# Two places instead of one for a block's token list and its indices

## The chip, the cores and the metric

The kernel runs on one core of a Trainium2 chip. The metric is the device time of one execution in microseconds (us).

## The reference, cut to what matters

A layer of deformable convolution attention is followed by a layer of linear attention with a mixture of experts. The change lies in the mixture of experts, the last part of the program: of four experts every token uses its best two.

```python
def _L1_ffn_ref(x, gate_w, gate_b, w1, b1, w2, b2):        # 4096 tokens of 384, 4 experts, 1536 hidden
    probs = softmax(einsum('bsd,de->bse', x, gate_w) + gate_b)
    topk_vals, topk_idx = top_k(probs, 2)
    mask = sum(one_hot(topk_idx, 4), axis=-2)
    masked = probs * mask
    masked = masked / (sum(masked, axis=-1, keepdims=True) + 1e-09)
    h = gelu(einsum('bsd,edh->ebsh', x, w1) + b1[:, None, None, :])
    y = einsum('ebsh,ehd->ebsd', h, w2) + b2[:, None, None, :]
    return einsum('bse,ebsd->bsd', masked, y)
...
t = t + _L1_ffn_ref(_ln_t(t), ...)
```

## The kernel before

The program has three stages. The first two are the convolution attention (to about 1390 us of the profile) and the linear attention with the gate (to about 1770 us). In `gate` each pair of a token and an expert gets a row of the table `tab_d` in DRAM, sorted by expert; a row holds the token's number to read from, the number to write to, and the gate's weight. The normalised tokens go to `tn_d`, the sum so far to `out`.

The third stage works on 25 blocks of rows of one expert each: 13 blocks of 512 rows, 3 of 256 and 9 of 128. `ORDER` says in which order: first ten long blocks, then two short ones (128 rows) and one long one in turn, then the rest. Which expert a block belongs to and where its rows begin is known only at run time; SP loads both from `btab`.

A block j passes through these steps:

- `fetch` (L1672) brings it in. SP issues, in this order, the loads of `en` (L1686, the rows of the table), w1 (L1700) and w2 (L1704, 2304 KB each), `b1c` (L1708) and `b2r` (L1710). POOL turns the first two columns of `en` into integers `ei` (L1690) and gathers the tokens `xr` with them by indirect DMA (L1693), 128 rows with each.
- `turn` (L1713) transposes the tokens: TensorE (`e_tr`, L1719), and VectorE copies the result to `d_xT` (L1722).
- `first_layer` (L2072) and the activation (L2079; for short blocks a copy, transposes `h_tr` and the activation, L2077, L2088 and L2092).
- `second_layer` (L2104) sums into PSUM banks `acc`, four for 512 rows. The pool has four banks.
- `rows_so_far` (L2117) gathers from `out` what these tokens have so far, by indirect DMA on POOL with `ei`, and VectorE adds the weighted bias (L2123, which reads `en` and `b2r`).
- `to_rows` adds the weighted result on VectorE (L2131, which reads `acc` and `en`) and POOL scatters the rows back to `out` (L2134, with `ei`). A token may have been written by a block before, so the gather at L2117 waits until the scatters of earlier blocks have landed.

There are three homes for blocks, (dw0, ds0), (dw1, ds1) and (dw2, ds2), used in turn. Each home has one place for every tile of `fetch`, so block j+2 takes over the places of block j-1. In the loop over the units (12 units of 128 hidden columns for a long block, 3 of 512 for a short one), `fetch` of block j+2 is written down in the second unit of block j (first unit if j is short), `turn` of block j+1 three units before the end of block j, and the first layer runs two units ahead of the second:

```python
                if u == (1 if n == HC else 0) and j + 2 < N_BLK:
                    ds[j + 2] = fetch(j + 2, *homes[(j + 2) % 3])
                if u == n - 3 and j + 1 < N_BLK:
                    turn(ds[j + 1], j + 1, d2p)
```

The order of instructions on each engine in this stage is set by a scheduler that goes by priorities and by when it expects operands and places to be free. Every engine then works off its own list in order, and waits at an instruction whose operands or whose place aren't ready; what stands behind it waits too.

Of the kernel before, what the change touches and what calls it, by code (L numbers as in the profile page):

```python
# [11 lines left out]
F32 = mybir.dt.float32  # L12
I32 = mybir.dt.int32
# [6 lines left out]
P = 128  # L20
# [131 lines left out]
def bc(ap, axis, n):  # L152

    dims = [list(d) for d in ap.ap]
    dims.insert(axis, [0, n])
    return bass.AP(ap.tensor, ap.offset, dims)
# [3 lines left out]
def body(  # L160
# [140 lines left out]
    with tc.tile_pool(name="a_w", bufs=1) as aw, tc.tile_pool(name="a_1", bufs=1) as a1, tc.tile_pool(  # L301
        name="a_2", bufs=2
    ) as a2, tc.tile_pool(name="a_3", bufs=2) as a3, tc.tile_pool(name="a_s", bufs=2) as asm, tc.tile_pool(
        name="a_cv", bufs=1, space=PSUM
    ) as pcv, tc.tile_pool(name="a_mm", bufs=2, space=PSUM) as pmm, tc.tile_pool(
        name="a_tr", bufs=3, space=PSUM
# [560 lines left out]
        def fetch(b, k):  # L867

            ga = a3.tile([P, G, 2, 2 * GC], F32, tag="ga", bufs=4, name=f"ga{b}_{k}")
            for g in range(G):  # L870
                nc.gpsimd.indirect_dma_start(  # L871
                    out=ga[:, g].rearrange("p s c -> p (s c)"),
                    out_offset=None,
                    in_=img[b][:, :],
                    in_offset=bass.IndirectOffsetOnAxis(
                        ap=pidxs[b, k][:, g : g + 1], axis=0
                    ),
                )
            gas[b, k] = ga
# [43 lines left out]
        for b in range(B):  # L923
# [56 lines left out]
            for f in range(2):  # L980
# [51 lines left out]
                for k in range(4 * f, 4 * f + 4):  # L1032
                    k0 = k // sizes[0] * sizes[0]
                    done = (k + 1) % sizes[0] == 0
                    step(
                        ("G", b, k), "Pool", 8.6, 1 + b + 0.01 * k, (lambda b=b, k=k: fetch(b, k)),
                        [("N", b, k0, 12), ("S", b, 16)] + [("rec", b, i) for i in range(2 * G)]
                        + [("G", b - 1, i) for i in range(NB) if b]
                        + [("G", b, i) for i in range(k0) if b == B - 2],
                        takes=[("ga", (b, k))], gives=[("pidx", (b, k0))] if done else [],  # L1040
                    )
                    step(("L", b, k), "queue", 0.0, 0, lambda: None, [("G", b, k)], lag=2.6)
                    step(
                        ("M", b, k), "DVE", 3.4, 2.2 + b, (lambda b=b, k=k: sampled(b, k)),
                        [("L", b, k), ("N", b, k0, 13)] + ([("M", b, k - 1)] if k % K4 else []),
                        takes=[(f"xs{b % 2}{f}", (b, f))] if k % K4 == 0 else [],
                        gives=[("ga", (b, k))] + ([("w4", (b, k0))] if done else []),
                    )
# [66 lines left out]
    with tc.tile_pool(name="b_w", bufs=1) as bwp, tc.tile_pool(name="b_qkv", bufs=2) as bq, tc.tile_pool(  # L1115
        name="b_win", bufs=4
    ) as bwin, tc.tile_pool(name="b_t", bufs=4) as bt, tc.tile_pool(name="b_o", bufs=2) as bo_, tc.tile_pool(
        name="b_s", bufs=6
    ) as bS, tc.tile_pool(name="b_m", bufs=2) as bm, tc.tile_pool(name="b_ao", bufs=1) as bao, tc.tile_pool(
        name="b_y", bufs=3  # L1120
# [377 lines left out]
        with tc.manual_schedule(  # L1498
# [22 lines left out]
            for g in range(NP + 7):  # L1521


                i, kp = divmod(g, KP)
# [51 lines left out]
            while waiting:  # L1576
                tag, n = spots.pop(0)
# [94 lines left out]
    def fetch(j, pool, small):  # L1672

        i = ORDER[j]
        b, size = blocks[i]
        why = "the table is made of clipped counts"
        e = nc.values_load(
            btab[0:1, i, 0:1], engines=SP, min_val=0, max_val=E_N - 1,
            skip_runtime_bounds_check_because=why,
        )  # L1680
        r = nc.values_load(
            btab[0:1, i, 1:2], engines=SP, min_val=0, max_val=ROWS - size,
            skip_runtime_bounds_check_because=why,
        )
        en = small.tile([P, 4, 4], F32, tag="en", name=f"en{i}")
        nc.sync.dma_start(  # L1686
            en[:, : size // P, :], tab_d[bass.DynSlice(r, size), :].rearrange("(p k) c -> p k c", p=P)
        )
        ei = small.tile([P, 4, 2], I32, tag="ei", name=f"ei{i}")
        nc.gpsimd.tensor_copy(ei[:, : size // P], en[:, : size // P, 0:2])  # L1690
        xr = small.tile([P, 4, NC], F32, tag="xr", name=f"xr{i}")
        for k in range(size // P):
            nc.gpsimd.indirect_dma_start(  # L1693
                out=xr[:, k, :],
                out_offset=None,
                in_=tn_d[: (b + 1) * N, :],
                in_offset=bass.IndirectOffsetOnAxis(ap=ei[:, k, 0:1], axis=0),
            )
        t1 = pool.tile([P, CK, HID], F32, tag="w1", name=f"w1_{i}")
        nc.sync.dma_start(  # L1700
            t1, w1[bass.DynSlice(e, 1)].rearrange("o (a p) d -> p (o a) d", p=P)
        )
        t2 = pool.tile([P, HC, NC], F32, tag="w2", name=f"w2_{i}")
        nc.sync.dma_start(  # L1704
            t2, w2[bass.DynSlice(e, 1)].rearrange("o (a p) d -> p (o a) d", p=P)
        )
        c1_ = small.tile([P, HC], F32, tag="b1c", name=f"b1c{i}")
        nc.sync.dma_start(c1_, b1_d[bass.DynSlice(e, 1)].rearrange("o p a -> (o p) a"))  # L1708
        r2 = small.tile([P, NC], F32, tag="b2r", name=f"b2r{i}")
        nc.sync.dma_start(r2, bc(b2[bass.DynSlice(e, 1)].rearrange("o c -> (o c)"), 0, P))  # L1710
        return dict(j=j, size=size, b=b, en=en, ei=ei, xr=xr, w1=t1, w2=t2, b1=c1_, b2=r2)
# [18 lines left out]
    with tc.tile_pool(name="c_1", bufs=1) as c1, tc.tile_pool(name="c_2", bufs=2) as c2, tc.tile_pool(  # L1730
        name="c_s", bufs=2
# [246 lines left out]
        def outputs(b):  # L1978
# [36 lines left out]
            if b == 1:  # L2015

                state["block"] = fetch(0, dw0, ds0)
# [36 lines left out]
    with tc.tile_pool(name="d_w1", bufs=1) as dw1, tc.tile_pool(name="d_s1", bufs=1) as ds1, tc.tile_pool(  # L2054
        name="d_w2", bufs=1
    ) as dw2, tc.tile_pool(name="d_s2", bufs=1) as ds2, tc.tile_pool(name="d_2", bufs=2) as d2p, tc.tile_pool(
        name="d_h", bufs=3
# [86 lines left out]

        homes = [(dw0, ds0), (dw1, ds1), (dw2, ds2)]
        ds = {0: first, 1: fetch(1, *homes[1])}
        units = []
        for j in range(N_BLK):
# [76 lines left out]
```

## Time and profile before

| | us |
|---|---|
| median of three runs | 2853.95 (2847.24 to 2855.77) |
| the profiled execution | 2848.14 |
| its span on the core | 2846.1 |
| TensorE busy | 2585.0 (91%) |
| VectorE busy | 1578.6 (55%) |
| ScalarE busy | 1158.2 (41%) |
| GpSimd (POOL) busy | 853.3 (30%) |

The profile is of one execution. Its own time is the span and what lies around it (2 us here), and is 5.8 us below the median of the three runs. Engines are PE (TensorE), PEld (its weight loads, which overlap PE), DVE (VectorE), ACT (ScalarE), POOL (GpSimd) and SP (SyncE, which only issues DMAs here). L1686 is line 1686 of the kernel. An arrow `ei<-en` gives output and input of an instruction; a bracket such as `[1.62 <-DMA xr<-tn_d,ei]` is the idle time of the engine before the instruction and what ended it. PEclk is the granted clock of TensorE as a share of full speed. The ends of matmuls are modelled; distances are better taken from start to start.

### The profile page before, as it was taken

How to read it: one execution, taken by the hardware profiler on the slowest of the kernel's cores; microseconds unless marked ns; L12 is line 12 of the kernel's file. 1: busy time of each engine (PE TensorE's matmuls, PEld its weight loads, DVE VectorE, ACT ScalarE, POOL GpSimd, SP SyncE). 2: the span in 40 equal slices, each digit the busy share in tenths (PEclk: the TensorE clock that was granted, in tenths of full speed). 3: DMA queues.
4: the chain of work that ended last, by engine and by line, in shares of the span. 5: the costliest groups of instructions: out<-in, count | busy, mean ns of one | idle time of the engine just before them, and what ended most of it. 6: DMA issues, size and time to landing. Idle time of an engine off the chain costs nothing. (4 is left out here: it accounts for less than half of the span.)

```text
span 2846.1 us, 33342 instructions
## 1 busy us (share of the span) xinstructions
PE 2585.0 (91%) x12731; PEld 1283.9 (45%) x12731; DVE 1578.6 (55%) x2349; ACT 1158.2 (41%) x1532; POOL 853.3 (30%) x776
## 2 busy tenths in 40 slices
PE   8899838898989988888799898999999999999999
PEld 5555512332333333233365554555555555555566
DVE  3888859999999999999656765000101011011011
ACT  5565536777667766676323322111111111111121
POOL 1668853232333333332112335211112111021121
PEclk9899969999999999999999999999999999999999
DMA  7934575454546555544121312622223434374371
GB/s 205 257 115 133 173 209 165 130 154 145 164 145 194 177 157 149 145 151 127 55 74 52 119 45 70 250 103 103 103 103 119 146 129 142 114 255 172 117 267 58
DMA packets 267899, 404.77 MB, mean 142 GB/s; under 512 B 134674, under 2 KB 207634, under 8 KB 267356
## 3 DMA queue, kind: packets, MB, share of 16 engines
q1 hardware_dynamic: 214912, 230.43, 25.6%
q0 software_dynamic: 52112, 172.15, 18.6%
q8 instruction: 100, 1.64, 0.2%
q14 instruction: 59, 0.48, 0.1%
q10 hardware_dynamic: 716, 0.07, 0.0%
HBM read 345.68 MB, written 70.06 MB: 146 GB/s over the span
## 5 line engine op out<-in xcount | busy, mean ns | idle before, releaser
L2072 PE MATMUL ph<-d_xT,w 128*128 128x512 f32 (+1 forms) x1152 | 484.1, 554 | 1.3 <-ACT h L2079 1.3
L2104 PE MATMUL acc<-w,h 128*128 128x384 f32 x1392 | 480.3, 486 | 0.0
L1168 POOL DMA_INDIRECT win<-table,widx x192 | 278.2, 1449 | 642.4 <-DVE t L1194 612.8
L1221 PE MATMUL ps<-q,k 64*64 64x512 f32 x1536 | 380.3, 608 | 91.6 <-DVE S L1252 43.4
L2079 ACT ACTIVATE h<-ph,b1c 128x512 f32<-128x512 f32 (+1 forms) x192 | 124.2, 647 | 776.2 <-PE ph L2072 761.7
L1226 PE MATMUL ps<-o,ident 64*64 64x512 f32 x1536 | 376.6, 609 | 9.4 <-ACT o L1202 9.4
L2104 PEld LDWEIGHTS acc<-w,h 128*128 128x128 f32 x1392 | 264.1, 190 | 208.5 <-issue 73.2
L2072 PEld LDWEIGHTS ph<-d_xT,w 128*128 128x128 f32 x1152 | 217.0, 191 | 196.3 <-issue 144.5
L871 POOL DMA_INDIRECT ga<-img,pidx x192 | 233.3, 1215 | 145.7 <-DVE gd L600 62.5
L2134 POOL DMA_INDIRECT out<-rows,ei x67 | 67.2, 1003 | 699.4 <-DVE rows L2131 690.5
L1315 ACT ACTIVATE S<-S 128x2048 f32<-128x2048 f32 x96 | 183.4, 1910 | 190.3 <-DVE S L1311 190.3
L1221 PEld LDWEIGHTS ps<-q,k 64*64 64x64 f32 x1536 | 98.8, 133 | 354.4 <-issue 211.3
L1722 DVE COPY d_xT<-e_tr 128x512 f32<-128x512 f32 (+2 forms) x75 | 36.6, 512 | 385.5 <-PE e_tr L1719 385.5
L1194 DVE SCALAR_TENSOR_TENSOR t<-win,bw,t 128x1056 f32<-128x1056 f32 x192 | 244.5, 1314 | 5.1 <-ACT t L1184 3.9
L1252 DVE SCALAR_TENSOR_TENSOR S<-t,bw,ps 128x1024 f32<-128x1024 f32 x192 | 236.9, 1275 | 17.4 <-PE ps L1226 14.3
L2123 DVE SCALAR_TENSOR_TENSOR rows<-b2r,en,rows 128x384 f32<-128x384 f32 x67 | 40.7, 618 | 361.3 <-DMA rows<-out,ei 311.1
L1184 ACT ACTIVATE t<-win,bw 128x1056 f32<-128x1056 f32 x192 | 218.1, 1168 | 40.3 <-DMA win<-table,widx 39.2
L1202 ACT ACTIVATE o<-t,bw 128x1024 f32<-128x1024 f32 x192 | 212.8, 1144 | 35.2 <-DVE t L1194 30.0
L1329 PE MATMUL po<-S,v 128*64 128x512 f32 x768 | 199.0, 642 | 24.4 <-ACT av L1354 13.9
L1311 DVE TENSOR_TENSOR S<-S,pbs 128x2048 f32<-128x2048 f32 x96 | 218.9, 2282 | 2.0 <-ACT pbs L1306 2.0
L2131 DVE SCALAR_TENSOR_TENSOR rows<-acc,en,rows 128x384 f32<-128x384 f32 x67 | 41.4, 618 | 217.6 <-PE acc L2104 215.7
L1270 DVE TENSOR_TENSOR m<-m,S 128x2048 f32<-128x2048 f32 x48 | 117.1, 2440 | 1.6
(350 smaller groups left out, 3441.8 us busy)
## 6 DMA issues: line engine op xcount, KB each, us to landing
w<-in_L_ffn_w SPq DMA_DIRECT2D x50, 2304.0 KB
img<-in_x SPq DMA_DIRECT2D x48, 256.0 KB
q<-q_d SPq DMA_DIRECT2D x48, 256.0 KB
x<-in_x SPq DMA_DIRECT2D x8, 768.0 KB
q_d<-qt SPq DMA_DIRECT2D x24, 256.0 KB
v_d<-qkvw SPq DMA_DIRECT2D x32, 192.0 KB
v<-v_d SPq DMA_DIRECT2D x24, 256.0 KB
k<-k_d SPq DMA_DIRECT2D x48, 128.0 KB
```

What stands on the lines that cost most here:

```text
L871: nc.gpsimd.indirect_dma_start(out=ga[:, g].rearrange("p s c -> p (s c)"), out_offset=None, in_=img[b][:, :], in_offset=bass.IndirectOffse ...
L1168: nc.gpsimd.indirect_dma_start(out=win, out_offset=None, in_=tables[h // 2][:, :], in_offset=bass.IndirectOffsetOnAxis(ap=widx[b][:, nb, h ...
L1184: nc.scalar.activation(t.rearrange("p y x -> p (y x)"), wins[p, e][:, : HI * WIN], AF.Copy, scale=weight(p, e, 0),)
L1194: nc.vector.scalar_tensor_tensor(tf, wins.pop((p, e))[:, WIN:], weight(p, e, 1), tf, ALU.mult, ALU.add)
L1202: nc.scalar.activation(o, ts[p, e][:, :, 0:WI], AF.Copy, scale=weight(p, e, 2))
L1221: made.append(nc.tensor.matmul(ps[HALF[1 - r], e, FULL[f]], k[HALF[r], 2 * kp + e, :], q[HALF[r], FULL[f]], start=(step == 0), stop=(step ...
L1226: made.append(nc.tensor.matmul(ps[HALF[r], d, FULL[f]], ident[HALF[r], HALF[r]], os_[p, d][HALF[r], FULL[f]], start=(step == 0), stop=(ste ...
L1252: nc.vector.scalar_tensor_tensor(st[:, e, :].rearrange("p (y x) -> p y x", x=WI), ts.pop((p, e))[:, :, 1:WIN], weight(p, e, 3), ps[:, e, : ...
L1311: nc.vector.tensor_tensor(Ss[p], Ss[p], bc(pbss[p // KP][:, :], 1, 2), ALU.add)
L1329: nc.tensor.matmul(pos[i][0][HALF[f], :], vs[i][:, 2 * kp + e, :], Ss[p][:, e, FULL[f]], start=(first and e == 0), stop=(last and e == 1),)
L2072: nc.tensor.matmul(ph if short(d) else ph[:, :n], a, m, start=(c == 0), stop=(c == CK - 1))
L2104: nc.tensor.matmul(d["acc"][0 if short(d) else s][:, :NC], h[:, s * P : (s + 1) * P], d["w2"][:, hc, :], start=(hc == 0), stop=(hc == HC - 1),
```

## The change

In `fetch`, the tiles `en` and `ei` get two places in each home instead of one. Everything else in a home (`xr`, w1, w2, `b1c`, `b2r`) keeps its one place. A home's `en` takes 64 bytes a partition and `ei` 32 bytes.

```diff
@@ fetch
-        en = small.tile([P, 4, 4], F32, tag="en", name=f"en{i}")
+        en = small.tile([P, 4, 4], F32, tag="en", bufs=2, name=f"en{i}")
         nc.sync.dma_start(
             en[:, : size // P, :], tab_d[bass.DynSlice(r, size), :].rearrange("(p k) c -> p k c", p=P)
         )
-        ei = small.tile([P, 4, 2], I32, tag="ei", name=f"ei{i}")
+        ei = small.tile([P, 4, 2], I32, tag="ei", bufs=2, name=f"ei{i}")
         nc.gpsimd.tensor_copy(ei[:, : size // P], en[:, : size // P, 0:2])
         xr = small.tile([P, 4, NC], F32, tag="xr", name=f"xr{i}")
         for k in range(size // P):
```

With two places, block j+2 uses the place that block j-4 had, while block j-1 keeps its own.

## The prediction

> **What bounds the kernel now.** I read the page first: busy shares, then the forty slices.
>
> ```profile
> PE 2585.0 (91%) x12731; PEld 1283.9 (45%) x12731; DVE 1578.6 (55%) x2349; ACT 1158.2 (41%) x1532; POOL 853.3 (30%) x776
> PE   8899838898989988888799898999999999999999
> ```
>
> TensorE has the largest share, and the last fifteen slices (from 1779 us on), in the stage of the experts' blocks, read 9 throughout. This stage runs on what `fetch` brings, the only function that the diff touches, so only TensorE's idle time there can be won. The waits of PE between 1760 and 2847 us (line that waited, what it waited for: us in total, times, longest) are a single line:
>
> ```profile
> PE e_tr L1719 <- DMA xr<-tn_d,ei: 11.4, 9, 2.3
> ```
>
> So weights are never late, PSUM banks are never late; only the gathered tokens `xr` are. The table of windows, two of 20 us and three of 2 us (length, PE, PEld, DVE, ACT, POOL busy, then PEclk, DMA share, GB/s) shows that the holes are also slow:
>
> ```profile
> 2500.00:2520.00 20.00, 17.37 (x57) 9.50 (x57) 3.31 (x5) 4.21 (x14) 8.15 (x10) 0.91 0.96 344
> 2520.00:2540.00 20.00, 20.00 (x59) 10.48 (x58) 1.24 (x2) 3.78 (x8) 5.66 (x7) 1.00 0.71 254
> 2509.60:2511.60 2.00, 1.02 (x3) 0.32 (x2) 0.34 (x1) 0.00 (x0) 1.02 (x1) 0.80 0.57 193
> 2511.60:2513.60 2.00, 1.97 (x7) 1.46 (x7) 1.24 (x2) 0.00 (x0) 0.00 (x0) 0.50 0.88 224
> 2513.60:2515.60 2.00, 2.00 (x8) 1.05 (x7) 0.74 (x2) 0.00 (x0) 1.42 (x3) 0.85 1.01 418
> ```
>
> There are four such holes, at 2406, 2508, 2610 and 2713 us: each at the turn of a long block (512 or 256 rows) that follows two short ones of 128 rows. The timeline around the second (start, duration, engine, line, operation) tells why `xr` is late:
>
> ```profile
> 2491.45 0.33 SPq L1686 DMA_DIRECT2D en<-tab_d  x1
> 2493.58 0.99 POOL L2134 DMA_INDIRECT out<-rows,ei  x1 [0.30 <-issue]
> 2501.36 0.19 POOL L1690 CAST ei<-en 128x8 int32<-128x8 f32 x1 [6.80 <-issue]
> 2502.09 1.00 POOL L2117 DMA_INDIRECT rows<-out,ei  x1 [0.54 <-issue]
> 2507.18 0.95 POOL L1693 DMA_INDIRECT xr<-tn_d,ei  x1 [0.30 <-issue]
> 2509.45 0.33 PE L1719 MATMUL e_tr<-ident,xr 128*128 128x128 f32 x1 [1.62 <-DMA xr<-tn_d,ei]
> 2512.80 1.72 PE L2072 MATMUL ph<-w,d_xT 128*128 128x512 f32 x2
> 2516.51 0.60 PE L2088 MATMUL h_tr<-ident,h 128*128 128x128 f32 x4
> ```
>
> The new block takes the home of the block that ended at about 2491. Its token list `en` cannot be loaded before that block's last DVE reader (L2131), its indices `ei` cannot be written before that block's last scatter has landed: POOL writes `ei` at 2501.36. Four gathers then need 5 us to issue and land while SP's weight transfers fill the DMA engines (share 0.96). TensorE is ready at 2507.67 (the last second-layer group starts at 2505.09, and such groups start 2.58 us before their follower). The queue of SP says the same for every block:
>
> ```profile
> SPq L1686 <- DVE rows L2131: 740.9, 22, 53.0
> ```
>
> **What the Trainium skill says.** "Perfetto Trace Analysis", section Optimization Strategy: the same gap repeating on the engine that should be saturated can mean that the next tile has no place yet. The trace agrees: four equal gaps, and the wait of L1686 above is for a place. "TensorE: Matmul & The Clock Gate", Part 1: after about one idle window of 3.4 us the clock falls to half until a window of that length has been busy. The trace agrees in part: 0.80, 0.50 and 0.85 in three windows of 2 us are 0.4 + 1.0 + 0.3 = 1.7 us lost, or 3.4 us at half speed; but here 2.5 us of idleness, broken by one transpose, was enough, and the first hole (3.1 us) shows 1.00 all along. "DMA: Bandwidth & Descriptors", section Queues, rings and completion order: on each DMA engine the descriptors of one issuing queue are consumed in ring order. So a small load issued behind weights on SP starts behind them. The trace agrees: `en` of the third block, issued at 1784.45 behind 4.6 MB of weights, lets POOL run at 1793.04, 8.6 us later.
>
> **The change, part by part.** Instructions, sizes and DMAs stay the same in number. Each home gets a second place for `en` (64 bytes a partition) and `ei` (32 bytes). I take these 288 bytes at nothing: no tile loses a place for them, and matmuls read the same tiles.
>
> What moves, by the order of instructions of the changed kernel: PE, DVE, ACT and SP issue the same sequence. On POOL, from the fourth block on, the cast and the gathers of `xr` of block j+3 stand behind the `rows` gathers of block j and ahead of its scatters; before, they stood behind these scatters and among the `rows` gathers of block j+1.
>
> (1) SP. The load of `en` no longer waits for L2131; it is issued as soon as `b2r` of the fetch ahead of it is out (2500.94 for the group shown, instead of the next block's 2510.07). SP then stands at w1 (L1700), whose place is free after the old block's last first-layer group, two units (about 10 us) ahead of that block's end, and at w2 until its end. w1 so starts about 12 us earlier, w2 2 to 3 us. Since PE never waits for weights, this wins nothing; nothing else is queued on SP.
>
> (2) POOL. The gathers of a long block now go out behind the `rows` gathers of the long block before it: for the turn at 2507.67 at about 2440 instead of 2503.40, 67 us ahead of their use instead of 4. Its landing takes 6.0 us in the median. The stall at L1719 goes.
>
> (3) What the stall costs. An undisturbed turn of the same kind, 12 transposes and 6 first-layer instructions, runs from 1804.28 to 1808.17: 3.89 us. The disturbed ones run 2406.26 to 2414.10 (7.84), 2507.67 to 2516.51 (8.84), 2610.07 to 2618.88 (8.81); the fourth, with 6 transposes (0.65 us) and the 6 others (2.58 us), 2712.44 to 2720.72 (8.28 instead of 3.23). Losses: 3.95 + 4.95 + 4.92 + 5.05 = 18.9 us. The wait's 11.4 us are part of it; the rest is the half clock (three times 1.7 = 5.1) and transposes that come one at a time.
>
> (4) What is late next. At a turn without the wait, the third group of transposes waits for DVE's copy (L1722) and fills with two first-layer instructions; that is in the 3.89. The weights of the long block were issued one block earlier. The bank of a short block's `acc` must be read by L2131 when the long block takes its four: L2123 ran at 2418.37 to 2418.99 in the first group, and the short block's PE work, ending at 2427.87, will end about 4 us sooner: 5 us remain.
>
> (5) The new wait. POOL's cast of block j+3 waits for its `en`, now behind weights, and holds the scatter of block j. In a short block: SP is past `b2r` at 2399.7, so `en` goes out at about 2400.4. Lower bound of its delay: about 2 us, as with the first `en` of the stage, without weights ahead (issued 1773.93, cast 1775.88). Upper bound: the 8.6 us above. I take 5, since w1 has started earlier. Even the upper end puts the cast at 2409.0 and the scatter, behind cast and one gather (0.2 + 0.3 + 1.0 us), at 2410.7 instead of 2408.16: 2.5 us, inside the 5 us. Cost zero; a gain beyond the 18.9 has no source in PE's waits.
>
> Sum: -18.9 us. The profiled execution took 2848.14 us (span 2846.1), so 2829.2 for one like it; the median of the runs is 5.8 us above it, 2853.95, which gives 2835. The last part (from 2820) is not touched and shifts as a whole.
>
> **The rivals.** About 0.3% (8.6 us) is what a measurement can tell from no change.
> Rival A, part of the gain: the wait is removed in some groups only, or the clock still falls at another small gap. If half remains, 2853.95 - 9.5 = 2844.5; if nothing but the clock's share is won, 5 us, 2849. For it: the DMA share is near 1.0 around each hole, so gathers land late there. Against it: the moved gathers fall into the long block, where the share is 0.39 from 2440 to 2460 us and 0.00 from 2460 to 2480.
> Rival B, the change doesn't do what it says: `xr` has one place still, and if its release or `tn_d` held the gathers, 2854. Against it: `xr` of the old block is read by the transposes one block before, and POOL's new order stands.
> Rival C, slower: `en` behind the weights holds POOL in front of the scatter (part 5), so `rows` of the next block, which must follow that scatter, come late, L2131 keeps the `acc` bank, and PE stops at L2104. It decides where the scatter slips by more than 5 us. To lose 8.6 us net over the eight short blocks of the four groups, 27.5 / 8 = 3.4 us each are needed, so 8.4 us of slip without a lost clock, 6.7 with 1.7 us of it: `en` landing 13 us or more after its issue, against 8.6 seen. That gives 2862.5.
>
> **How the numbers follow.** Main case 0.76: 2835, with 8 us to each side for the spread of the runs (2847 to 2856 before). A 0.11, B 0.05, C 0.08. The range starts at 2827 and reaches over most of A to 2851; beyond it lie C, part of B and little else. Faster by over 0.3% is the main case and the better part of A: 0.80; the same, the rest of A and B: 0.12; slower 0.08.
>
> **What would show it.** Right: no line PE L1719 <- DMA `xr` after 1760 us, clock 1.00 there, SP's L1686 waiting no longer for L2131 but L1700 and L1704 for PE, and POOL's casts waiting for `en` by under 9 us. Wrong: PE waiting at L2104 or L2072, DVE's L2131 running behind L2123 in short blocks by more than a microsecond, or `e_tr` still waiting for `xr`.

## The result, and the profile after

The changed kernel takes 2839.31 us (median of six runs, 2832.19 to 2841.2) against 2854.86 us for the kernel before on the same chip (six runs, 2847.24 to 2855.97): 15.5 us less, a ratio of 0.9945 with a 95% interval of 0.993 to 0.9961. The forecast was 2835 us, from 2827 to 2851. The profiled execution took 2841.2 us, span 2839.5.

The busy times and the slices of TensorE on the page of the changed kernel:

```profile
PE 2589.1 (91%) x12731; PEld 1282.9 (45%) x12731; DVE 1578.9 (56%) x2349; ACT 1158.2 (41%) x1532; POOL 857.2 (30%) x776
PE   8899838898899889889799898999999999999999
```

The shares stay as they were, to a point; a stall of 19 us in 2840 doesn't show at this resolution. It shows in the waits of PE from 1740 us on (line that waited, what for: us in total, times, longest). Two of the lines belong to the experts' blocks. Both lie ahead of the first L2131, where the kernel before waits at the same two lines (1.3 us each). The line of L1719 waiting for the gathers `xr` (11.4 us before) is gone:

```profile
PE ph L2072 <- ACT h L2079: 1.3, 1, 1.3
...
PE e_tr L1719 <- DVE d_xT L1722: 0.9, 1, 0.9
```

The windows across the second group of two short blocks and a long one (length, PE, PEld, DVE, ACT, POOL busy, then PEclk, DMA share, GB/s): PE is full, at full clock, although the DMA share is as high as before.

```profile
2500.00:2520.00 20.00, 20.00 (x75) 11.38 (x74) 3.30 (x6) 5.13 (x16) 5.15 (x6) 1.00 0.97 338
2520.00:2540.00 20.00, 20.00 (x59) 10.60 (x59) 1.24 (x2) 4.49 (x12) 3.15 (x4) 1.00 0.91 319
```

The timeline of PE at the first turn of a long block in these groups (start, duration, engine, line, operation): eight transposes in one go, two first-layer instructions, four more transposes, the rest.

```profile
2418.03 1.04 PE L1719 MATMUL e_tr<-ident,xr 128*128 128x128 f32 x8
2418.90 1.02 PE L2072 MATMUL ph<-w,d_xT 128*128 128x512 f32 x2
2419.84 0.66 PE L1719 MATMUL e_tr<-ident,xr 128*128 128x128 f32 x4
2420.33 1.88 PE L2072 MATMUL ph<-w,d_xT 128*128 128x512 f32 x4
2422.05 0.60 PE L2088 MATMUL h_tr<-ident,h 128*128 128x128 f32 x4
```

From 2418.03 to 2422.05 are 4.02 us, where it had been 7.84. The other three turns take 3.89, 3.89 and 3.59 us, after 8.84, 8.81 and 8.28. Gain: 3.82 + 4.95 + 4.92 + 4.69 = 18.4 us.

The same figure comes from a second measure, which I use for all experiments: the **stage** of the blocks, from the start of the first L2131 to that of the last (the instruction's durations in ns, then these two starts in us; before, then after):

```profile
L2131 DVE SCALAR_TENSOR_TENSOR rows<-acc,en,rows x67: 616/618/619, 1819.3 to 2841.3; 128x384 f32<-128x384 f32 x67
L2131 DVE SCALAR_TENSOR_TENSOR rows<-acc,en,rows x67: 616/617/620, 1831.1 to 2834.7; 128x384 f32<-128x384 f32 x67
```

It took 1022.0 us before and 1003.6 us after, 18.4 us less. So outside the four turns nothing in the stage gained or lost more than a few tenths of a microsecond. The spans differ by only 6.6 us (2846.1 and 2839.5) since the stages ahead of the blocks, which have no changed line, took 11.8 us longer in the execution profiled after. That is their spread: a second execution of the changed kernel has its first L2131 at 1826.0.

SP's waits are what the change acts on. Before, L1686 stood 740.9 us for L2131. After, L1686 has left this list except for the first table load of the stage, and the queue stands at the weights:

```profile
SPq L1700 <- PE ph L2072: 583.0, 15, 46.7
SPq L1704 <- PE acc L2104: 161.7, 14, 13.2
SPq L1704 <- PE e_tr L1719: 103.3, 8, 13.2
```

POOL's timeline in the first group (in brackets the idle time before, and what ended it):

```profile
2411.44 0.99 POOL L2117 DMA_INDIRECT rows<-out,ei  x1 [6.49 <-DMA out<-rows,ei]
2413.75 0.19 POOL L1690 CAST ei<-en 128x2 int32<-128x2 f32 x1 [1.32 <-DMA en<-tab_d]
2414.51 0.98 POOL L1693 DMA_INDIRECT xr<-tn_d,ei  x1 [0.58 <-POOL ei L1690]
2419.47 1.02 POOL L2134 DMA_INDIRECT out<-rows,ei  x1 [3.97 <-DVE rows L2131]
2427.40 0.98 POOL L2117 DMA_INDIRECT rows<-out,ei  x1 [6.91 <-DMA out<-rows,ei]
2430.19 0.19 POOL L1690 CAST ei<-en 128x2 int32<-128x2 f32 x1 [1.82 <-DMA en<-tab_d]
```

The cast now stands ahead of the scatter L2134 and waits for `en` behind weights, as forecast. But the scatter isn't held up by it: it waits another 3.97 us for L2131 of its own block. What did become slower is the scatter's landing. The next gather L2117 follows 6.91 us after the scatter's end. In the kernel before it had been the cast that followed, 1.86 us after it:

```profile
2411.04 0.18 POOL L1690 CAST ei<-en 128x2 int32<-128x2 f32 x1 [1.86 <-DMA out<-rows,ei]
```

So `rows` of the second short block come later. DVE's timeline there, after the change:

```profile
2433.85 0.62 DVE L2123 SCALAR_TENSOR_TENSOR rows<-b2r,en,rows 128x384 f32<-128x384 f32 x1 [12.62 <-DMA xr<-tn_d,ei]
2436.02 0.62 DVE L2131 SCALAR_TENSOR_TENSOR rows<-acc,en,rows 128x384 f32<-128x384 f32 x1 [1.56 <-PE acc L2104]
```

L2123 ends only 1.6 us before `acc` is ready; in the kernel before, 9.1 us. The fourth bank is wanted a little later still: of the eight second-layer instructions of the long block (start 2438.39, one each 0.32 us), six run on free banks, so the need comes at about 2440.3, and L2131 ends at 2436.64. Together 1.6 + 3.7 = 5.3 us are left in this group.

### The profile page after: what moved, and what is told of

The parts are those of the page before. It is cut to its first block, busy times and chain, and to the rows that moved or that the text cites. A ratio compares the mean times of both kernels' runs of the same rounds, so it can differ in the third digit from the quotient of the medians.

```text
span 2839.5 us, 33345 instructions
## 1 busy us (share of the span) xinstructions
PE 2589.1 (91%) x12731; PEld 1282.9 (45%) x12731; DVE 1578.9 (56%) x2349; ACT 1158.2 (41%) x1532; POOL 857.2 (30%) x776
## 4 chain that ended last, share of the span: by engine, by line
PE 55%; DVE 21%; issue 9%; POOL 7%; DMA 5%; ACT 3%; SPq 0%; DVEq 0%; POOLq 0%; ACTq 0%
PE ph L2072 16%; PE acc L2104 16%; PE ps L1221 6%; DVE S L1252 6%; POOL ga L871 5%; DVE t L1194 5%; PE c_kv L1951 3%; DVE S L1311 3%; DVE m L1270 3%; PE c_y L2022 2%; PE po L1329 1%; PE po L1338 1%; DMA ga<-img,pidx 1%; PE pcv L713 1%; DMA out<-rows,ei 1%
## 5 line engine op out<-in xcount | busy, mean ns | idle before, releaser
L2104 PE MATMUL acc<-w,h 128*128 128x384 f32 x1392 | 480.3, 486 | 0.0
L1221 PE MATMUL ps<-q,k 64*64 64x512 f32 x1536 | 386.8, 617 | 91.0 <-DVE S L1252 43.5
L2079 ACT ACTIVATE h<-ph,b1c 128x512 f32<-128x512 f32 (+1 forms) x192 | 124.2, 647 | 776.2 <-PE ph L2072 761.7
L1226 PE MATMUL ps<-o,ident 64*64 64x512 f32 x1536 | 383.1, 618 | 9.7 <-ACT o L1202 9.7
L2104 PEld LDWEIGHTS acc<-w,h 128*128 128x128 f32 x1392 | 264.1, 190 | 208.5 <-issue 73.2
L1722 DVE COPY d_xT<-e_tr 128x512 f32<-128x512 f32 (+2 forms) x75 | 36.3, 510 | 432.0 <-PE e_tr L1719 431.8
L2134 POOL DMA_INDIRECT out<-rows,ei x67 | 67.2, 1004 | 639.4 <-DVE rows L2131 630.3
L2123 DVE SCALAR_TENSOR_TENSOR rows<-b2r,en,rows 128x384 f32<-128x384 f32 x67 | 41.3, 618 | 326.7 <-DMA rows<-out,ei 300.2
L2131 DVE SCALAR_TENSOR_TENSOR rows<-acc,en,rows 128x384 f32<-128x384 f32 x67 | 41.4, 617 | 187.5 <-PE acc L2104 185.9
```

The costliest lines, as they stand in the source:

```text
L1221: made.append(nc.tensor.matmul(ps[HALF[1 - r], e, FULL[f]], k[HALF[r], 2 * kp + e, :], q[HALF[r], FULL[f]], start=(step == 0), stop=(step ...
L1226: made.append(nc.tensor.matmul(ps[HALF[r], d, FULL[f]], ident[HALF[r], HALF[r]], os_[p, d][HALF[r], FULL[f]], start=(step == 0), stop=(ste ...
L2104: nc.tensor.matmul(d["acc"][0 if short(d) else s][:, :NC], h[:, s * P : (s + 1) * P], d["w2"][:, hc, :], start=(hc == 0), stop=(hc == HC - 1),
```

## The experiments

The stage and the times of each kernel:

| kernel | stage, us | median, us | kernel before on that chip, us | ratio (95% interval) |
|---|---|---|---|---|
| again | 1003.5 | 2835.79 | 2857.65 | 0.9925 (0.9912 to 0.9939) |
| en_only | 1024.1 | 2854.56 | 2857.65 | 0.9991 (0.9982 to 0.9999) |
| ei_only | 1007.3 | 2839.68 | 2857.65 | 0.9936 (0.9922 to 0.9949) |
| pad | 1023.7 | 2857.45 | 2857.65 | 1.0 (0.9991 to 1.0008) |
| alt_one | 1002.9 | 2888.23 | 2916.56 | 0.9903 (0.9867 to 0.9939) |
| alt_two | 1002.8 | 2889.33 | 2916.56 | 0.9894 (0.9849 to 0.994) |
| hold2 | 1003.5 | 2900.38 | 2916.56 | 0.9942 (0.9918 to 0.9966) |
| hold6 | 1005.2 | 2900.54 | 2916.56 | 0.9944 (0.992 to 0.9968) |
| tt4 | 1015.8 | 2899.06 | 2918.4 | 0.9942 (0.9918 to 0.9967) |
| tt6 | 1023.8 | 2911.1 | 2918.4 | 0.9975 (0.9957 to 0.9992) |
| again2 | 1003.6 | 2893.01 | 2918.4 | 0.9913 (0.9881 to 0.9944) |
| alt_two2 | 1002.8 | 2894.28 | 2918.4 | 0.9916 (0.9893 to 0.9938) |

The kernels of a chip share its runs of the kernel before. Where the lower eight ran, the whole took 2% longer and runs scatter by 10 us and more. What is longer there is the part ahead of the blocks (first L2131 at 1865.2 us or later, against 1831.1 or earlier in the upper four and the two kernels compared); the stage isn't, so it is the better measure.

### Which of the two tiles matters, and whether the addresses do

Four kernels on one chip. The first is the changed kernel as it is (again). The next two do half of the change, and pad gives the one place of `en` 160 bytes instead of 64, so that what lies behind moves while no place is added:

```diff
# en_only, against the kernel before
-        en = small.tile([P, 4, 4], F32, tag="en", name=f"en{i}")
+        en = small.tile([P, 4, 4], F32, tag="en", bufs=2, name=f"en{i}")
# ei_only, against the kernel before
-        ei = small.tile([P, 4, 2], I32, tag="ei", name=f"ei{i}")
+        ei = small.tile([P, 4, 2], I32, tag="ei", bufs=2, name=f"ei{i}")
# pad, against the kernel before
-        en = small.tile([P, 4, 4], F32, tag="en", name=f"en{i}")
+        en = small.tile([P, 10, 4], F32, tag="en", name=f"en{i}")
```

> The changed kernel once more. My theory: the four stalls at the turns of long blocks cost 18.9 us in the profile of before and nothing now, and the stages ahead of the blocks only differ by chance between executions, so the ratio lies between 0.9930 (-19.9 us) and 0.9945 (-15.7 us), nearer to 0.9935. The rival: the 96 bytes in each home shift other tiles and make the earlier stages some 3 us slower for good, so it stays at 0.9945 or above.

> Two places for en alone, one for ei. My theory: the cast into ei still waits until the scatter of the old block has landed, and the gathers of xr stay where they were, so most of the stall stays: 0 to -6 us (the weights start earlier, so the gathers may land a little sooner). The rival that the early start of SP's loads is the win: -15 us or more, and no line PE L1719 waiting for xr.

> Two places for ei alone, one for en. My theory: en is loaded at the old block's end as before (about 2 us), but the cast no longer waits for the scatter to land (6 to 7 us), so the gathers go out some 8 us earlier, against stalls of 2.5 to 3.2 us: most of the win is there, -12 to -19 us, with small waits of PE for xr possible. The rival that both places are needed: under -6 us.

> One place for both, en made 96 bytes a partition larger: the same addresses behind it as in the changed kernel, and the same order of instructions as before. My theory: no difference, 0 within 2 us. The rival of shifted tiles: +3 us.

**pad** is as fast as the kernel before, to 0.1%, and PE's wait is still there. Addresses are no cause. Its stage of 1023.7 us is 1.7 us longer than the 1022.0 us in the profile before, because the clock was at half for four stretches of 3.4 us (one from 2514.3, two from 2616.7, one from 2722.5) instead of three (from 2510.8, 2613.2 and 2715.6).

```profile
PE e_tr L1719 <- DMA xr<-tn_d,ei: 11.3, 11, 2.2
```

**en_only** frees SP and wins nothing in the stage (1024.1 us). Its waits, of PE and then of POOL, are those of the kernel before: the cast stands until the old block's scatter has landed.

```profile
PE e_tr L1719 <- DMA xr<-tn_d,ei: 11.1, 11, 1.6
...
POOL ei L1690 <- DMA out<-rows,ei: 112.7, 20, 6.6
```

The ratio puts the total 2.6 us lower, with an interval that just excludes none; since the stage isn't shorter, I don't count it as won by the change.

**ei_only** leaves SP where it was, standing at L1686, and wins 16.4 us of the stage against pad, of 20.2 for both places. Its waits, PE's and then SP's:

```profile
PE e_tr L1719 <- DVE d_xT L1722: 3.6, 3, 1.6
...
SPq L1686 <- DVE rows L2131: 698.9, 22, 51.7
```

POOL's timeline in its second group tells how the gain comes:

```profile
2499.60 0.98 POOL L2134 DMA_INDIRECT out<-rows,ei  x1 [0.30 <-issue]
2500.57 0.22 POOL L1690 CAST ei<-en 128x8 int32<-128x8 f32 x1
2501.07 1.00 POOL L1693 DMA_INDIRECT xr<-tn_d,ei  x1 [0.28 <-POOL ei L1690]
```

The cast follows the old block's scatter at once. It doesn't wait until that scatter has landed, and the four gathers go out ahead of the next L2117 (2508.21), the first of them 12.6 us ahead of the turn (2513.69); in the kernel before it was 4.3 us (2503.40 to 2507.67). So the place that was missing is that of `ei`, which stays in use until the scatter has landed.

The last 3.8 us (1007.3 against 1003.5) have a cause of their own. PE's turn in ei_only waits for DVE's copies,

```profile
2513.69 1.04 PE L1719 MATMUL e_tr<-ident,xr 128*128 128x128 f32 x8
2514.57 1.02 PE L2072 MATMUL ph<-w,d_xT 128*128 128x512 f32 x2
2516.68 0.66 PE L1719 MATMUL e_tr<-ident,xr 128*128 128x128 f32 x4 [1.09 <-DVE d_xT L1722]
```

and these copies stand on DVE behind the short block's L2123, which waits for its `rows`:

```profile
2514.68 0.62 DVE L2123 SCALAR_TENSOR_TENSOR rows<-b2r,en,rows 128x384 f32<-128x384 f32 x1 [16.43 <-DMA rows<-out,ei]
2515.41 0.62 DVE L2131 SCALAR_TENSOR_TENSOR rows<-acc,en,rows 128x384 f32<-128x384 f32 x1
2515.94 1.28 DVE L1722 COPY d_xT<-e_tr 128x512 f32<-128x512 f32 x2
```

In ei_only the gathers of `xr` stand ahead of this `rows` gather on POOL. The turn takes 5.20 us (2513.69 to 2518.89) instead of 3.89; with the two that follow (5.03 and 5.06 instead of 3.89 and 3.59) that is 3.9 us. With both places the `xr` of this block has been gathered a block earlier.

### Whether the stall comes from the order of the blocks

If the gathers of a long block are late because two short ones lie ahead of it, an order with one short block at a time must not have the stall, with one place or with two.

```diff
# alt_one: against the kernel before; alt_two and alt_two2: against the changed kernel
-ORDER = [0, 1, 2, 3, 4, 5, 6, 7, 8, 9, 16, 17, 10, 18, 19, 11, 20, 21, 12, 22, 23, 13, 14, 15, 24]
+ORDER = [0, 1, 2, 3, 4, 16, 5, 17, 6, 18, 7, 19, 8, 20, 9, 21, 10, 22, 11, 23, 12, 13, 14, 15, 24]
```

> The kernel before (one place each) with another ORDER: short and long blocks in turn from the sixth block on, so that no long block follows two short ones. My theory: the gathers of a long block's tokens then go out at the start of a long block, 62 us ahead of its turn, and no turn waits; about -19 us as with the two places, although SP's L1686 still waits for L2131 at every block. The rival that the early release of the places is worth something at every block: no gain without the second places, within 5 us of before.

> The changed kernel (two places each) with the same other ORDER. My theory: equal to alt_one within 3 us, since the second places have nothing left to win; -19 us. The rival: the two gains add, -30 us or more.

The only wait of L1719 in alt_one:

```profile
PE e_tr L1719 <- DVE d_xT L1722: 1.0, 1, 1.0
```

That wait lies ahead of the first L2131. With one place each, and with SP still standing 719.1 us at L1686, there is no wait for `xr`: the stage takes 1002.8 to 1002.9 us, with one place or with two. So the change takes away a stall that exists only at a long block behind two short ones.

The medians gain 28 and 27 us, more than the 19 expected, but with intervals of 18 to 39 and 17 to 44 us they can't tell 19 from the 30 of the rival. So the two versions without the stall were compared once more, on one chip:

> The changed kernel as it is, for comparison on the same chip: 0.9925 to 0.9945 of the kernel before, 15 to 21 us faster.

> The changed kernel with short and long blocks taken in turn rather than two short ones before each long one. Its stage of blocks took 1002.8 us against 1003.5 of the changed kernel. If the stall at xr is all that the order of blocks costs, the two differ by under 2 us here. Rival (the order has a cost of its own ahead of the stage, in the first fetches, or a gain, as 0.9894 on another chip hints): 5 us or more between them, in either direction.

The medians are 2893.01 and 2894.28 us, the stages 1003.6 and 1002.8 us. Within the spread they are the same (the rival had asked for 5 us), and neither order nor places brings more on top of the other.

### How much room the scatter has

The rival that ends slower says that POOL, held at the cast, lets the scatter slip until PE stands at L2104 for a bank. To make it slip, POOL gets work of its own right behind the cast of a block below 512 rows, in the changed kernel. What it writes is overwritten by the gathers.

```diff
# hold2 (2), hold6 (6): copies
+        for _ in range(6 if size < 512 else 0):
+            nc.gpsimd.tensor_copy(xr, bc(bc(en[:, 0, 0], 1, 4), 2, NC))
# tt4 (4), tt6 (6): additions
+        for _ in range(6 if size < 512 else 0):
+            many = bc(bc(en[:, 0, 0], 1, 4), 2, NC)
+            nc.gpsimd.tensor_tensor(xr, many, many, ALU.add)
```

> The changed kernel with 2 extra copies of 1536 elements on POOL behind the cast in fetch of every block of under 512 rows, into xr before the gather overwrites it: some 3 to 4 us more between cast and scatter. My theory: POOL has about 4 us to spare ahead of the scatter of a short block (cast and gather end at 2415.5, scatter at 2419.5 in the profile after), so the gain stays, -15 to -21 us.

> The same with 6 extra copies, some 10 to 12 us between cast and scatter. My theory (rival C of the prediction made to happen): the scatter slips by 6 to 8 us, of which about 1.5 us are covered in front of L2131; PE then stops at L2104 for acc once in each group with two short blocks, some 5 us each with the clock's fall after it, and most of the gain is gone: 0 to -8 us. The rival that scatters of short blocks have time to spare: the gain stays.

hold2 takes the 1003.5 us of the changed kernel. hold6 takes 1.7 us more, all at the turns of the four groups (4.49, 4.46, 4.24 and 3.86 us, with 1.1 us of waits for DVE's copies), and has no wait for a bank. The gain stays, 16.0 us, where 0 to 8 were expected. Its POOL timeline in the first group:

```profile
2448.08 9.29 POOL L1693 COPY xr<-en 128x1536 f32<-128x1536 f32 x6
2457.51 1.01 POOL L2136 DMA_INDIRECT out<-rows,ei  x1 [0.15 <-issue]
```

and DVE's (L2125 and L2133 are L2123 and L2131 here):

```profile
2453.10 0.62 DVE L2133 SCALAR_TENSOR_TENSOR rows<-acc,en,rows 128x384 f32<-128x384 f32 x1
...
2469.13 1.79 DVE L2125 SCALAR_TENSOR_TENSOR rows<-b2r,en,rows 128x384 f32<-128x384 f32 x1 [13.38 <-DMA rows<-out,ei]
2471.03 0.62 DVE L2133 SCALAR_TENSOR_TENSOR rows<-acc,en,rows 128x384 f32<-128x384 f32 x1
```

Six copies took 9.3 us, so the scatter slips by 3.5 us (2453.72 to 2457.51, less the 0.3 us it takes anyway). L2133 of the second short block now runs right behind L2125, some 0.5 us after its `acc` is ready. That goes the way of the sign that the prediction named for the slower case, which asked for more than a microsecond. The bank is free at 2471.65 for a need at 2474.85: 3.2 us are left. The hold was too small to decide.

> The changed kernel with four additions of 1536 elements on POOL behind the cast of a short block's fetch, so ahead of the scatter of the block that is then being worked on. One of 384 elements took 1.0 us on POOL (L2013), so an addition is estimated at 3.9 us and the four at 15.6. With six copies (9.3 us) the scatter slipped by 3.5 us and about 3 us were left before TensorE needed the bank. Theory (the scatter's slip sets when L2131 frees the acc bank; it decides from some 6.5 us on): slip about 10 us, TensorE waits about 3.5 us at L2104 for L2131 in each of the four groups, perhaps with the clock's 1.7 us: the time is 14 to 21 us above the changed kernel, so 2 us faster to 5 us slower than the kernel before. Rival (the scatter isn't what frees the bank, or other slack lies behind it): no wait of PE, 15 to 20 us faster than before, as with the six copies.

> The same with six additions, an estimated 23 us. Theory: slip about 17.5 us, TensorE waits about 11 us at L2104 in each of the four groups and falls to half clock once or twice in each: 45 to 60 us above the changed kernel, so 28 to 42 us slower than the kernel before, with a line of PE acc L2104 waiting for DVE L2131, and that line stands behind L2123 in short blocks by more than a microsecond. Rival (other slack): under 15 us above the changed kernel and no such line.

An addition took 2.8 us (2.74 to 2.95), not 3.9, so the holds are 11.4 and 17 us. **tt4** has no wait for a bank, and is 12.2 us slower in the stage all the same. PE's waits are

```profile
PE e_tr L1722 <- DVE d_xT L1725: 8.9, 5, 3.2
```

and DVE's timeline at the last of them is

```profile
2799.65 5.58 DVE L2126 SCALAR_TENSOR_TENSOR rows<-b2r,en,rows 128x384 f32<-128x384 f32 x2 [12.18 <-DMA rows<-out,ei]
2805.15 0.74 DVE L1725 COPY d_xT<-e_tr 128x256 f32<-128x256 f32 x2
2806.35 0.42 DVE L1725 COPY d_xT<-e_tr 128x256 f32<-128x256 f32 x1 [0.45 <-PE e_tr L1722]
```

Two instructions of 0.62 us each take 5.58 us while POOL adds (2799.05 to 2810.66), and PE waits for the copy behind them. The clock is then at half from 2804.7 to 2811.5 us, which costs some 3 us more; with the 8.9 us of waits that is nearly all of the 12.2. So tt4 met a cost of the experiment's own: its loss is at DVE's copies and not at the bank. Its median, 19 us below the kernel before, lies in the range that the expectation gave to its rival, and confirms nothing.

**tt6** has the same (8.4 us at L1722), and in one group, the second, what the rival describes. Its waits of PE:

```profile
PE e_tr L1722 <- DVE d_xT L1725: 8.4, 5, 2.7
PE acc L2107 <- DVE rows L2134: 6.2, 1, 6.2
```

The chain, from the timelines of POOL, DVE and PE (L2137, L2120, L2126, L2134 and L2107 are L2134, L2117, L2123, L2131 and L2104 here):

```profile
2582.76 1.01 POOL L2137 DMA_INDIRECT out<-rows,ei  x1 [0.15 <-issue]
2584.08 0.98 POOL L1696 DMA_INDIRECT xr<-tn_d,ei  x1 [0.30 <-issue]
2589.03 0.96 POOL L2120 DMA_INDIRECT rows<-out,ei  x1 [3.97 <-DMA out<-rows,ei]
```

```profile
2596.60 2.34 DVE L2126 SCALAR_TENSOR_TENSOR rows<-b2r,en,rows 128x384 f32<-128x384 f32 x1 [22.30 <-DMA rows<-out,ei]
2599.05 0.62 DVE L2134 SCALAR_TENSOR_TENSOR rows<-acc,en,rows 128x384 f32<-128x384 f32 x1
```

```profile
2591.47 2.10 PE L2107 MATMUL acc<-w,h 128*128 128x384 f32 x6
2599.72 1.65 PE L2107 MATMUL acc<-w,h 128*128 128x384 f32 x2 [6.15 <-DVE rows L2134]
```

and the windows in which PE resumes:

```profile
2599.00:2601.00 2.00, 1.28 (x2) 0.83 (x3) 0.62 (x1) 0.00 (x0) 2.00 (x1) 0.50 0.19 57
2601.00:2603.00 2.00, 2.00 (x4) 0.84 (x3) 0.00 (x0) 0.00 (x0) 1.92 (x2) 0.56 0.16 46
```

Six instructions of the long block run, the two on the fourth bank wait 6.15 us for L2134, and the clock is at half for some 3.0 us after it (0.50 and 0.56 in the windows), which costs another 1.5. From the last L2134 of the long block before to that of this group's long block, the run loses 8.7 us against the changed kernel; 0.9 of it is a wait at L1722.

In each of the three groups that end with a block of 512 rows the scatter goes out 10.5 us after its L2134 has ended (in the first: 2473.65 and 2484.14), and in the first and the third PE doesn't wait. There the path from the scatter's issue to L2126 takes 6.5 and 7.0 us; in the second it takes 13.8 (2582.76 to 2596.60), of which the gather is 7.6. SP issues a transfer of w2 0.06 us after that gather (2589.09), in the other two 2.9 and 2.5 us after it. The slip alone doesn't decide, then; it needs a slow landing too. That w2 makes it slow is argued from these times only, no run moved it.

So the rival's mechanism exists, with the line that the prediction gave it. It needs POOL to be held for 17 us, and even then it came in one group of three. The expected 45 to 60 us above the changed kernel were wrong: it is 20.2 us in the stage and 18.1 in the medians, and 11.5 of the 20.2 lie elsewhere, at turns that wait for DVE's slowed work and in two more stretches of half clock behind them (from 2780.3 and 2821.2).

## Why the prediction was right

**What bounds the kernel.** Right: the gathers `xr` were the only wait to be won, and pad, en_only and again show that wait and the gain go together. One reading was too short: the four gathers need 7.3 us, not 5, from the first issue (2503.40) to 2510.66, where PE's last wait for them ends.

**Step 1, SP.** Right. `en` leaves the wait for L2131, SP stands at w1 and w2 instead, and en_only shows that this by itself wins nothing in the stage.

**Step 2, POOL.** Right, with a share that the text left open: it named both the load of `en` and the landed scatter as what held the cast. ei_only shows that the scatter was the one that ended last: 16.4 of 20.2 us come with the second place of `ei`.

**Step 3, the stall's price.** 18.9 us expected, 18.4 found, by turns and by the stage. The missing 0.5 us is in two terms: the first turn takes 4.02 instead of 3.89 us and the fourth 3.59 instead of 3.23. In both, DVE's copies run right behind L2123 and L2131 of the short block (L2131 at 2418.57 and 2711.11), as in ei_only, only less late. That the size fits so closely is in part luck. The half clock was priced three times 1.7 us, as this execution had it; in pad it is four times, and against pad the gain is 20.2 us.

**Step 4, what is late next.** Half right. At the bank, 5 us was close to the 5.3 us that remain, but by another account: the scatter's landing took about 4 us more than before, which the prediction didn't have, and the bank is needed only 3.7 us after L2131's end, which it didn't count. And the bank is not what is late next. DVE's copies of the turn are, behind L2123 of the short block: there is no room there at all in the first turn after the change nor in the fourth, and ei_only, hold6, tt4 and tt6 all lose at that place before any bank is late. The prediction took the wait for L1722 as part of an undisturbed turn and didn't ask what stands ahead of the copies on DVE. The sign "L2131 running behind L2123 by more than a microsecond" stands once in the changed kernel: in the fourth group L2131 starts at 2727.66, right behind L2123 and 2.2 us after the block's last second-layer matmul. PE doesn't wait there; the next block has 256 rows and needs two of the four banks.

**Step 5, the new wait.** The delay of `en` was mis-sized: taken as 5 us and at most 8.6 from issue to cast, it is 9.9 us in the first short block (2403.85 to 2413.75) and 9.2 at 2626.75. A second error made up for it: `en` was taken to go out at 2400.4, 5.9 us ahead of the turn at 2406.26, but it goes out 14.2 us ahead of it (2403.85 for a turn at 2418.03), mostly since `b1c`, which held SP for 7.0 us there before, now takes 0.7. So the cast comes 4.3 us ahead of the turn, where 0.9 us ahead to 2.7 us after it had been reckoned. The cost of nothing holds, in part by luck: the cast waits at most 3.4 us after POOL has come to it in these groups, and the scatter waits another 1.9 to 5.2 us for L2131 after the cast and gather are out. The sign "casts waiting for `en` by under 9 us" failed by its letter: the longest is 11.2 us, at the stage's first fetches, where the kernel pad, with one place, has 10.4 too.

**The sum.** From its own profile 2829.2 us was forecast, and 2841.2 measured: 0.5 us of the difference is step 3, 11.8 us are the unchanged stages ahead, which were longer in that execution, less 0.3 us around the span. The allowance of 8 us for the spread of runs was of the right order: the gain in the medians is 15.5, 21.9 (again) and 25.4 us (again2), the last two a little beyond what was expected of them, while the stage agrees to 0.1 us in all three.

**The rivals.** A and B are excluded by the stage's 18.4 us. C is real but not reached: in the changed kernel the scatters of short blocks wait for L2131 and not for POOL's cast, and 17 us of work on POOL were needed to bring the wait for a bank about once. Its point of decision, a slip of 5 us, was too simple: slips of 10.5 us cost no bank wait in two places and 6.15 us in a third.

## What to carry to other kernels

In this program an index tile that a scatter reads stays in use until the scatter has landed (POOL's casts stood 112.7 us for that in en_only), so a next gather whose indices are written to the same place is tied to that landing; a second place of a few bytes unties them. Before adding places, look which reader of the old tile ends last: here the indices' second place alone brought 16.4 us of the stage and the token list's alone nothing, though it brought 3.8 us on top. And before calling the room behind a cured stall large, look on every engine what its next instruction stands behind: the bank had 5 us here, the copies on DVE none.

## What the runs showed of the hardware

I had not expected that work on POOL would slow DVE, and had overlooked that the Trainium skill says so: by "SBUF — State Buffer", section SBUF: two separate sides, a DVE operation with two inputs in SBUF and a GpSimd operation that reads SBUF exclude each other for a whole instruction. The trace agrees. L2126 has both inputs in SBUF; 0.62 us long elsewhere, it took 2.79 us on average in tt4 and 2.34 in tt6 while POOL added (an addition lasts 2.74 us), and 1.79 us in hold6 while it copied (1.5 us a copy). L2134, whose other input is the PSUM bank, took its 0.62 us at 2599.05 in tt6 while POOL added from 2590.13 to 2607.18. Over the whole of tt4, L2126 took up to 3.75 us and L2134 never more than 0.62.

The granted clock changes in steps of 3.41 us that lie at fixed places in an execution: in the kernel before it falls at 2510.78, 2613.18 and 2715.58 us, 30 such steps apart, and stays at 0.50 for one step each time. It goes with how long PE was busy in the step just before. In the stage, over the profiles of all kernels here, the clock fell after each of the 14 steps in which PE was busy for 0.66 to 1.52 us, and after none with 1.73 us or more. So a step needn't be idle, and a hole that lies across two steps can pass: in the kernel before the clock fell after 0.91 us of work (2507.37 to 2510.78), but not at the first hole, with 1.78 and 1.96 us (2404.97 to 2408.38 to 2411.79). The limits are those of modelled ends of matmuls. In tt6, after 1.03 us of work from 2592.54 to 2595.95, the clock was at half for two steps, through the rest of PE's 6.15 us without work and the first 3.0 us after it, and 1.00 from then on.

A scatter of 128 rows let its follower go 1.9 us after the end of its issue where w1 and w2 were issued 0.8 and 1.4 us after it started (before: 2408.16, 2408.91 and 2409.54), and 6.9 us after it where w2 was issued 1.3 us ahead of it (after: 2418.22 and 2419.47). It holds for all the single scatters of short blocks that POOL waited for: seven in the kernel before, 1.6 to 3.0 us, with the weights issued 0.7 to 1.8 us after the scatter started, and seven in the changed one, 5.8 to 7.7 us, with w2 issued 0.9 to 1.3 us ahead of it. en_only, in which SP's loads move and POOL's casts still wait for the scatter, has 5.1 to 6.6 us with w2 0.9 to 1.8 us ahead. Five in tt4 and tt6 with no weights issued from 8 us before to 4 us after took 1.7 to 2.0 us.

SP's issue of `b1c` took 6.1 to 8.5 us where both weight transfers were issued directly ahead of it (22 in a row in the kernel before, from 1820 us on), and 0.4 to 3.0 us where w1 had been issued 7 to 14 us earlier (the last 22 after the change). SP's waits put the difference down to ACT (L1708 waiting for L2079 and L2092), but `b1c` has one place in every kernel here, and the issues are short in en_only (0.7 to 2.1 us) and long in ei_only (6.1 to 10.4). It follows the order of SP's transfers; what holds the issue stays open.
